# A two-layer attention kernel: its matmuls cut into narrow column tiles

## The chip, the cores and the metric

The kernel runs on one core of a Trainium2 chip. The metric is the device time of one launch, in microseconds. A core has five engines that run side by side and wait for each other by semaphores: TensorE multiplies matrices (in the profile PE for the matmuls and PEld for the loads of their stationary operands), VectorE (DVE), ScalarE (ACT) and GpSimd (POOL) work element by element, and SyncE (SP) starts transfers. A matmul computes lhsT.T @ rhs: lhsT is the stationary operand, loaded first, and rhs the moving one, streamed past it. TensorE's array has 128 rows (the contraction) and 128 columns (the output partitions). A matmul that needs fewer rows or columns can be placed in a part of the array. "128x32" in this text is such a tile: 128 rows by 32 columns. [...]

## The reference

The input x has 128 rows (called s) of 256 tokens with 256 channels each, in float32. Two layers are applied, each as x = x + attention(groupnorm(x)), with attention inside each row s.

```python
# layer 0: 8 heads of 32 channels
bias = einsum('nijz,zh->nhij', pair_repr, bias_proj)
gate = sigmoid(x @ gate_proj)
q, k, v = split(x @ qkv_proj, 3)
sim = softmax(q @ k.T * scale) + bias
out = ((sim @ v) * gate) @ out_proj
# layer 1: 4 heads of 64 channels, keys within 16 of the query only
q, k, v = split(x @ w_in.T + b_in, 3)
scores = where(|i - j| <= 16, q @ k.T / sqrt(64), -inf)
out = (softmax(scores) @ v) @ w_out.T + b_out
```

The group norm before each layer has 32 groups, and its mean and variance are taken over all rows, tokens and the group's channels, so layer 1 can't begin before layer 0 has finished its last row.

## The kernel before, in words

The kernel holds a row as two halves of 128 channels by 256 tokens and computes with channels on partitions. It has three parts: a start that computes the pair bias and the statistics of x; layer 0; and layer 1. A guarded third path that computes everything again with shifted exponents is there for extreme inputs; it isn't entered with these inputs.

**Products of weights and rows.** A product of a 256x256 weight matrix with a row of 256 tokens is four 128x128 blocks over 256 columns. For the projections q, k, v and the gate of layer 0, and q, k and the output projection of layer 1, the kernel takes two rows together and needs seven block products instead of eight, with sums of weight blocks (`Quarters`) and sums of row blocks (`row_sums`). Class `Seven` (L573) does this in layer 0, and `two_of_them` (L616) interleaves two of them, q with k or v with gate, over one row stage each. Class `Summed` (L648) does it in layer 1, and `in_turn` (L687) interleaves q, k and the output projection of an earlier row pair. Both come through `product` at L594, or at L598 for v of layer 0, where the row is the stationary operand and the weights move. `one_by_one` (L702) is the plain four-block product, used for the output projection of layer 0 (po) and for the last rows of layer 1.

**Layer 0, one row stage** (the loop over s at L913): `scores(s, 0)` (L777) multiplies keys with queries for four heads, each in 32 rows of the array, with 128 keys as columns; `sum_heads` (L822) sums the exponents of the previous row (zs) and multiplies the bias with the values (bv); `attend` (L853) multiplies the exponents with the values (av); both go through `products` (L808) as 128x32 tiles, a head each. Then come `scores(s, 1)` for the other four heads and a `stretch` (L885) with 14 block products of the next row pair and the four of po. ScalarE takes the exponents and copies projections out of PSUM, VectorE forms sums, the reciprocal, the norm of rows to come and the residual, GpSimd the block sums.

**Layer 1, one stage of two rows** (the loop at L1256): `scores` (L1055) for both rows in 64x64 tiles, each with 64 keys and the 96 queries near them; `attend` (L1086) multiplies with the values, also 64x64, and sums the exponents into zs with `place` (L979) as 64x32 tiles; `stretch` (L1022) has 21 block products; `values` (L1037) computes v for two rows to come, in 128x64 tiles of 64 tokens. `sums` (L1125) copies the two half sums and adds them; `inverse` takes the reciprocal in three pieces between other VectorE work; `by_transfer` (L1146) sends it to DRAM and back, spread over partitions (1near); `divide` (L1170) multiplies it in (1at).

**What sets the order.** In both layers the order on TensorE, ScalarE and VectorE is that of the program (a manual schedule), in layer 1 also on GpSimd and SyncE. A float32 matmul appears in the profile as two loads and two matmuls, so every count on TensorE is twice that of the calls. [...]in layer 0 five form a ring that projections and scores share (`psum(banks0, "0", 5, 0)`), in layer 1 four, beside two for av and two for zs.

Of the kernel before, what the change touches and what calls it, by code (L numbers as in the profile page):

```python
# [9 lines left out]
F32 = mybir.dt.float32  # L10
AF = mybir.ActivationFunctionType
ALU = mybir.AluOpType
# [27 lines left out]
def conv_preact_kernel(  # L40
# [59 lines left out]
    def strip(a):  # L100
        return slice(B * a, B * (a + 1))
# [464 lines left out]
    def row_sums(t, x, engine):  # L566
# [3 lines left out]
        engine.tensor_tensor(t[:, 2], x[:, 3], x[:, 2], ALU.subtract)  # L570
        engine.tensor_tensor(t[:, 3], x[:, 1], t[:, 1], ALU.subtract)

    class Seven:  # L573


        def __init__(self, pool, weights, x, t, name, tag, by_token=False):
            self.weights, self.x, self.t, self.by_token, self.name = weights, x, t, by_token, name
# [7 lines left out]
        def product(self, n, two=None, first=False):  # L585
            x, t = self.x, self.t
            moving = {1: x[:, 0], 2: x[:, 1], 3: x[:, 3], 4: t[:, 3], 5: t[:, 0], 6: t[:, 1], 7: t[:, 2]}[n]
            out = two if n == 2 else self.ps[:, 1 if n in (3, 5) else 0, :]

            first = first or n == 1  # L590
            flags = dict(stop=n in (2, 3, 4), skip_group_check=True)
            weights = self.weights.stationary(n)
            if not self.by_token:
                nc.tensor.matmul(out, lhsT=weights, rhs=moving, start=first, **flags)  # L594
                return
            for t2 in range(2):
                cols = slice(t2 * P, (t2 + 1) * P)
                nc.tensor.matmul(out[:, cols], lhsT=moving[:, cols], rhs=weights, start=first and t2 == 0, **flags)  # L598

        def take(self, what):  # L600
            if what == "15":
# [44 lines left out]
            p.add_mid()  # L646

    class Summed(Seven):  # L648

# [47 lines left out]
            if n in (1, 5):  # L699
                amid(n)  # L700

    def one_by_one(w, at, name, done):  # L702

        ps = proj_bank(name)
        done(ps)
        for m in range(2):
            for kt in range(2):
                nc.tensor.matmul(  # L708
                    ps[:, m, :], lhsT=w[:, kt, m * P : (m + 1) * P], rhs=at[:, kt, :],
                    start=(kt == 0), stop=(kt == 1),  # L710
                )
                yield
# [10 lines left out]
    with ExitStack() as both:  # L723
# [20 lines left out]
        with ExitStack() as lay0:  # L744
# [32 lines left out]
            def scores(s, half):  # L777
                i, r = divmod(s, 2)
                q, k = res["q", i], res["k", i]
                sims = [sim_bank(f"sim{s}_{half}_{j}") for j in range(4)]  # L780
                for kt in range(2):
                    for j in range(4):
                        p0 = D0 * j
                        nc.tensor.matmul(  # L784
                            sims[j][:, kt, :],
                            lhsT=k[p0 : p0 + D0, 2 * r + half, kt * P : (kt + 1) * P],
                            rhs=q[p0 : p0 + D0, 2 * r + half, :],
                            start=True, stop=True,
                        )
                ex = att.tile([P, 4, 2, R], F32, tag="ex", name=f"ex{s}_{half}", bufs=4)  # L790
                both = att.tile([P, 4, R], F32, tag="both", name=f"both{s}_{half}")
                hd[s, half] = (ex, both)


                def weigh(js):
                    for j in js:
                        nc.scalar.activation(ex[:, j], sims[j], AF.Exp, scale=1.0 / math.sqrt(D0))  # L797

                weigh(range(3))
                return lambda: weigh((3,))  # L800
# [84 lines left out]
            def stretch(names, i, s, rest=lambda: None):  # L885

                po = iter(())
                if s >= 0:
                    po = one_by_one(out_sb, st[s]["at"], f"po{s}", lambda ps: st[s].update(po=ps))
                if 2 * i >= S:  # L890
                    rest()
                    for _ in po:
                        pass
                    return
                f, g = (
                    Seven(row, quarters[w], xns[i], tss[i], f"{w}{i}", w, by_token=(w == "v")) for w in names
                )
                for w, p in zip(names, (f, g)):
                    res[w, i] = p.to
                two_of_them(row, f, g, f"{names}{i}", po, rest)  # L900


            with tc.manual_schedule(engines={mybir.EngineType.PE, mybir.EngineType.Activation, mybir.EngineType.DVE}):
# [54 lines left out]
                for s in (S - 2, S - 1):  # L958
                    if s == S - 1:
                        keep_on(4)  # L960
                    for _ in one_by_one(out_sb, st[s]["at"], f"po{s}", lambda ps: st[s].update(po=ps)):
                        pass
                    finish(s)
                mean1, rstd1 = channel_columns(st1, most1, 1, keep_on)
# [4 lines left out]


        with ExitStack() as lay:
            ps_av = psum(lay, "1", 4, 0)
            row = lay.enter_context(tc.tile_pool(name="row1", bufs=4))
            att = lay.enter_context(tc.tile_pool(name="att1", bufs=2))
            st, hd, outs = {s: {} for s in range(S)}, {}, {}
# [38 lines left out]
            def project(s):  # L1014

                if s < 0:
                    return iter(())
                return one_by_one(w_out_t, st[s]["at"], f"1po{s}", lambda ps: st[s].update(po=ps))

            ats, ats_t, outputs, last_ots = {}, {}, {}, {}  # L1020

# [15 lines left out]
            def values(s):  # L1037
                if s >= S:
                    return
                i, r = divmod(s, 2)  # L1040
                ps = proj_bank(f"p1v{s}").rearrange("p a (b c) -> p (a b) c", c=P)
                for b in range(NB):
                    for kt in range(2):
                        for half in range(2):
                            nc.tensor.matmul(  # L1045
                                ps[KB * half : KB * (half + 1), b, :],
                                lhsT=xns[i][:, 2 * r + kt, KB * b : KB * (b + 1)],
                                rhs=w_in_t[:, kt, 2 * C + P * half : 2 * C + P * (half + 1)],
                                start=(kt == 0), stop=(kt == 1),
                            )  # L1050
                v = row.tile([P, NB, P], F32, tag="v", name=f"1v{s}")
                nc.scalar.copy(v, ps)  # L1052
                st[s]["v"] = v
# [32 lines left out]
            def attend(i):  # L1086

                if i < 0:
                    return

                if i < S // 2 - 1:
                    av = ps_av.tile([P, 2, 2, R], F32, tag="av", name=f"1av{i}", bufs=1)
                    av = [av[:, half] for half in range(2)]
                else:
                    av = [proj_bank(f"1av{i}_{half}") for half in range(2)]
                zs = ps_av.tile([P, 2, 2, R], F32, tag="zs", name=f"1zs{i}", bufs=1)
                zps = []
                for r in range(2):
                    (p, zp), v = hd.pop(2 * i + r), st[2 * i + r]["v"]
                    zps.append(zp)  # L1100
                    for b in range(NB):
                        for half in range(2):
                            for j in range(2):
                                keys, cols = slice(KB * half, KB * (half + 1)), slice(D1 * j, D1 * (j + 1))
                                q0, p0 = QLO[b], R * (b % 2) + QLO[b]

                                nc.tensor.matmul(  # L1107
                                    av[half][cols, r, q0 + QIN[b].start : q0 + QIN[b].stop],
                                    lhsT=v[keys, b, cols],
                                    rhs=p[keys, j, p0 + QIN[b].start : p0 + QIN[b].stop],  # L1110
                                    start=(r == 0 and b == 0), stop=(b == NB - 1),
                                    skip_group_check=True,
                                )

                for r in range(2):
                    for half in range(2):
                        for j in range(2):
                            keys = slice(KB * half, KB * (half + 1))
                            nc.tensor.matmul(
                                zs[strip(2 * j + r), half, 0, :], lhsT=place[keys, :], rhs=zps[r][keys, j, :],  # L1120
                                start=True, stop=True,
                            )
                hd["av", i] = (av, zs)

            def sums(i):  # L1125
                if i < 0:
                    return
                zs = hd["av", i][1]
                z = att.tile([P, R], F32, tag="z", name=f"1z{i}")
                nc.scalar.copy(z, zs[:, 0, 0, :])  # L1130
                nc.vector.tensor_tensor(z, zs[:, 1, 0, :], z, ALU.add)
                rz = att.tile([P, R], F32, tag="rz", name=f"1rz{i}")
                near = att.tile([P, 2, 2, R], F32, tag="near", name=f"1near{i}", bufs=1)
                hd["z", i] = (z, rz, near)
# [388 lines left out]
```

## Time and profile before

| | |
|---|---|
| Time before, median of 3 runs | 3169.02 us (3168.06 to 3169.51) |
| Span of the profiled execution | 3173.6 us |
| Instructions | 87,645, of them 36,859 matmuls and as many weight loads |
| Busy: PE, PEld | 98%, 75% |
| Busy: DVE, ACT, POOL | 81%, 59%, 51% |
| Mean granted TensorE clock | 0.991 |
| Row stages of layer 0 | from about 240 to 2080 us of the span |
| Stages of layer 1 | from about 2110 to 3145 us |

The profile is of one execution, whose own time is its span; it is 4.6 us longer than the median of the runs. A line of the timeline gives the start, the length, the engine, the source line, the operation, the output and its inputs, the rows and columns of the array that it uses, the shape of the moving operand and the count. Lengths of matmuls overlap, since a matmul starts before the one ahead has left the array; the time that a block takes is therefore read from its start to the next block's start.

### The profile page before, as it was taken

To read this page: it belongs to the slowest core of one execution; us is meant where nothing else is said; L and a number is where in the kernel's file an instruction comes from. 1 tells how busy PE (TensorE), PEld (TensorE's weight loads), DVE (VectorE), ACT (ScalarE), POOL (GpSimd) and SP (SyncE) were. 2 spreads that over 40 slices of the span, in tenths; PEclk is the share of its full clock that TensorE was granted. 3 is DMA by queue.
4 is the path that set the end of the run, shared out by engine and by line. 5 is a ranking of instruction groups with operands and counts; after the bars stand their busy time and mean duration, and the time that the engine had idled before them with its cause. 6 is when DMAs were issued, how large, how long until landed. Compare 5 with 4: busy or idle time off the path is not lost.

```text
span 3173.6 us, 87645 instructions
## 1 busy us (share of the span) xinstructions
PE 3097.4 (98%) x36859; PEld 2384.0 (75%) x36859; DVE 2558.2 (81%) x4140; ACT 1870.3 (59%) x4064; POOL 1613.4 (51%) x1651
## 2 busy tenths in 40 slices
PE   7889999999999999999999999999999999999997
PEld 5567777777777777777777777768888888888886
DVE  4669999999999999999999999956666666666665
ACT  4656666666666666666666666645555555555553
POOL 3034444444444444444444444347777777777774
PEclk8989999999999999999999999999999999999999
DMA  9931111111111111111111111004444444444343
GB/s 379 424 109 42 41 41 34 41 35 39 37 35 41 35 39 37 38 38 35 41 34 37 39 37 39 28 28 102 96 101 101 93 99 102 100 97 101 91 100 69
DMA packets 357105, 242.44 MB, mean 76 GB/s; under 512 B 276072, under 2 KB 342112, under 8 KB 350560
## 3 DMA queue, kind: packets, MB, share of 16 engines
q1 hardware_dynamic: 355808, 234.39, 27.1%
q8 instruction: 292, 4.78, 0.6%
q0 software_dynamic: 752, 2.36, 0.2%
q14 instruction: 109, 0.89, 0.1%
q10 hardware_dynamic: 144, 0.00, 0.0%
HBM read 169.09 MB, written 67.62 MB: 75 GB/s over the span
## 4 chain that ended last, share of the span: by engine, by line
PE 91%; DMA 5%; DVE 2%; ACT 1%; issue 0%; POOL 0%; SPq 0%; DVEq 0%; POOLq 0%; ACTq 0%
PE sim L784 9%; PE p1v L1045 7%; PE po L708 7%; PE av L816 7%; PE bv L816 7%; PE p1q L594 6%; PE pv L598 6%; PE p1o L594 6%; PE pq L594 6%; PE p1k L594 6%; PE pk L594 5%; PE pg L594 5%; DMA pr<-in_L_conv_pair_repr_dram 4%; PE zs L830 4%; PE 1sim L1066 3%; PE 1av L1107 3%
## 5 line engine op out<-in xcount | busy, mean ns | idle before, releaser
L797 ACT ACTIVATE ex<-sim 128x512 f32<-128x512 f32 x1024 | 547.5, 605 | 429.9 <-PE sim L784 429.9
L806 DVE TENSOR_TENSOR both<-ex 128x512 f32<-128x512 f32 x512 | 483.9, 984 | 77.0 <-ACT ex L797 77.0
L846 DVE RECIPROCAL d<-d 128x512 f32<-128x512 f32 x128 | 429.2, 3353 | 4.4
L611 POOL TENSOR_TENSOR v<-v,twovg 128x256 f32<-128x256 f32 x64 | 75.4, 1179 | 548.0 <-ACT twovg L630 548.0
L784 PE MATMUL sim<-q,k 32*128 32x256 f32 x4096 | 295.7, 401 | 1.1 <-ACT ex L797 1.1
L708 PE MATMUL po<-at,out_sb 128*128 128x256 f32 x1024 | 285.0, 382 | 4.0 <-DVE at L864 4.0
L784 PEld LDWEIGHTS sim<-q,k 32*128 32x128 f32 x4096 | 186.7, 184 | 102.4 <-issue 95.0
L816 PE MATMUL bv<-bias_sb,v 128*32 128x256 f32 x4096 | 244.5, 379 | 0.7 <-DVE t L861 0.7
L816 PE MATMUL av<-ex,v 128*32 128x256 f32 x4096 | 244.5, 379 | 0.0
L1045 PEld LDWEIGHTS p1v<-w_in_t,1xn 128*64 128x64 f32 x4096 | 222.3, 137 | 21.5 <-PE p1k L594 20.2
L1045 PE MATMUL p1v<-w_in_t,1xn 128*64 128x128 f32 x4096 | 237.7, 274 | 0.3 <-POOL place L980 0.3
L1076 POOL TENSOR_TENSOR 1p<-1ex,seen 128x768 f32<-128x768 f32 x127 | 230.9, 1818 | 13.4 <-ACT 1ex L1074 13.4
L668 ACT ACTIVATE 1q<-p1q,bqk 128x256 f32<-128x256 f32 x192 | 91.1, 474 | 244.4 <-PE p1q L594 244.4
L708 PEld LDWEIGHTS po<-at,out_sb 128*128 128x128 f32 x1024 | 185.7, 191 | 25.4 <-issue 4.3
L1176 DVE TENSOR_TENSOR 1at<-1av,1near 128x512 f32<-128x512 f32 x128 | 82.6, 686 | 148.6 <-DMA 1near<-rz_far 116.7
L816 PEld LDWEIGHTS bv<-bias_sb,v 128*32 128x32 f32 x4096 | 133.2, 110 | 88.7 <-issue 1.1
L611 POOL TENSOR_TENSOR q<-q,twoqk 128x256 f32<-128x256 f32 x64 | 47.6, 744 | 298.5 <-ACT twoqk L630 298.5
L816 PEld LDWEIGHTS av<-ex,v 128*32 128x32 f32 x4096 | 133.2, 110 | 87.8 <-issue 0.3
L766 DVE TENSOR_SCALAR xn<-xt,mean,rstd 128x256 f32<-128x256 f32 x256 | 179.9, 742 | 0.0
L1083 POOL TENSOR_TENSOR 1zp<-1p 128x512 f32<-128x512 f32 x127 | 162.1, 1276 | 10.0
L568 POOL TENSOR_TENSOR 1ts<-1xn 128x256 f32<-128x256 f32 x64 | 47.0, 734 | 234.3 <-ACT 1xn L1006 234.3
L1052 ACT COPY 1v<-p1v 128x512 f32<-128x512 f32 x128 | 75.1, 587 | 135.1 <-PE p1v L1045 131.6
(300 smaller groups left out, 7872.4 us busy)
## 6 DMA issues: line engine op xcount, KB each, us to landing
pr<-in_L_conv_pair_repr_dram SPq DMA_DIRECT2D x32, 1024.0 KB
xs<-in_x_dram SPq DMA_DIRECT2D x16, 2048.0 KB
x<-o SPq DMA_DIRECT2D x64, 512.0 KB
yg<-x SPq DMA_DIRECT2D x64, 512.0 KB
out_dram<-1o SPq DMA_DIRECT2D x256, 128.0 KB
xg<-in_x_dram SPq DMA_DIRECT2D x252, 128.0 KB
1near<-rz_far SPq DMA_DIRECT2D x124, 256.0 KB
rz_far<-1rz SPq DMA_DIRECT2D x124, 4.0 KB
```

Source lines behind the costliest of these rows:

```text
L594: nc.tensor.matmul(out, lhsT=weights, rhs=moving, start=first, **flags)
L598: nc.tensor.matmul(out[:, cols], lhsT=moving[:, cols], rhs=weights, start=first and t2 == 0, **flags)
L708: nc.tensor.matmul(ps[:, m, :], lhsT=w[:, kt, m * P : (m + 1) * P], rhs=at[:, kt, :], start=(kt == 0), stop=(kt == 1),)
L766: nc.vector.tensor_scalar(xns[i][:, 2 * r + half, :], xt[:, half, :], mean0[:, half : half + 1], rstd0[:, half : half + 1], op0=ALU.subtra ...
L784: nc.tensor.matmul(sims[j][:, kt, :], lhsT=k[p0 : p0 + D0, 2 * r + half, kt * P : (kt + 1) * P], rhs=q[p0 : p0 + D0, 2 * r + half, :], sta ...
L797: nc.scalar.activation(ex[:, j], sims[j], AF.Exp, scale=1.0 / math.sqrt(D0))
L806: nc.vector.tensor_tensor(both[:, j : j + 2], ex[:, j : j + 2, 0, :], ex[:, j : j + 2, 1, :], ALU.add)
L816: nc.tensor.matmul(to[D0 * j : D0 * (j + 1), half, :], lhsT=v[:, 2 * r + half, c0 : c0 + D0], rhs=weights(4 * half + j, kt), start=(kt == ...
L846: nc.vector.reciprocal(d, d)
L1045: nc.tensor.matmul(ps[KB * half : KB * (half + 1), b, :], lhsT=xns[i][:, 2 * r + kt, KB * b : KB * (b + 1)], rhs=w_in_t[:, kt, 2 * C + P * ...
L1076: engine.tensor_tensor(p.rearrange("p j (r c) -> p (j r) c", c=WROW)[:, :, 0 : 2 * WSTEP] .rearrange("p r (t c) -> p r t c", c=WSTEP)[:, : ...
L1083: engine.tensor_tensor(zp, p[:, :, 0:R], p[:, :, R : 2 * R], ALU.add)
```

## The change

All products of weights and rows in both layers are issued as four matmuls of 32 columns each, one after another, instead of one of 128 columns. A new function does it, and `Seven.product`, hence also `Summed`, and `one_by_one` call it with a width of 32 (`B`).

```diff
+    def in_columns(out, lhsT, rhs, width, **flags):
+        for c0 in range(0, P, width):
+            cols = slice(c0, c0 + width)
+            nc.tensor.matmul(out[cols], lhsT=lhsT[:, cols], rhs=rhs, **flags)
...
             if not self.by_token:
-                nc.tensor.matmul(out, lhsT=weights, rhs=moving, start=first, **flags)
+                in_columns(out, weights, moving, self.WIDTH, start=first, **flags)
                 return
...
-                nc.tensor.matmul(out[:, cols], lhsT=moving[:, cols], rhs=weights, start=first and t2 == 0, **flags)
+                in_columns(out[:, cols], moving[:, cols], weights, self.WIDTH, start=first and t2 == 0, **flags)
...
-                nc.tensor.matmul(
-                    ps[:, m, :], lhsT=w[:, kt, m * P : (m + 1) * P], rhs=at[:, kt, :],
+                in_columns(
+                    ps[:, m, :], w[:, kt, m * P : (m + 1) * P], at[:, kt, :], width,
                     start=(kt == 0), stop=(kt == 1),
                 )
```

The scores of layer 0 take 64 keys as columns instead of 128, so that eight tiles of 32x64 fill the array where four of 32x128 did.

```diff
                 for kt in range(2):
-                    for j in range(4):
-                        p0 = D0 * j
-                        nc.tensor.matmul(
-                            sims[j][:, kt, :],
-                            lhsT=k[p0 : p0 + D0, 2 * r + half, kt * P : (kt + 1) * P],
+                    for c in range(2):
+                        for j in range(4):
+                            p0, k0 = D0 * j, kt * P + KB * c
+                            nc.tensor.matmul(
+                                sims[j][KB * c : KB * (c + 1), kt, :],
+                                lhsT=k[p0 : p0 + D0, 2 * r + half, k0 : k0 + KB],
```

In layer 1 the values take 32 tokens as columns instead of 64, and the sums of the exponents use all 128 rows at once, with both halves of the keys, so that the addition of two half sums on VectorE goes. The sums then need one bank of PSUM instead of two, and the ring for projections and scores has five banks instead of four. The scores and the products with the values in layer 1 stay 64x64.

```diff
-            ps_av = psum(lay, "1", 4, 0)
+            ps_av = psum(lay, "1", 5, 0)
...
-                        for half in range(2):
+                        for n in range(A):
+                            half, keys = n // 2, KB * b + B * (n % 2)
                             nc.tensor.matmul(
-                                ps[KB * half : KB * (half + 1), b, :],
-                                lhsT=xns[i][:, 2 * r + kt, KB * b : KB * (b + 1)],
+                                ps[strip(n), b, :],
+                                lhsT=xns[i][:, 2 * r + kt, keys : keys + B],
...
-                zs = ps_av.tile([P, 2, 2, R], F32, tag="zs", name=f"1zs{i}", bufs=1)
+                zs = ps_av.tile([P, 2, R], F32, tag="zs", name=f"1zs{i}", bufs=1)
...
-                    for half in range(2):
-                        for j in range(2):
-                            keys = slice(KB * half, KB * (half + 1))
-                            nc.tensor.matmul(
-                                zs[strip(2 * j + r), half, 0, :], lhsT=place[keys, :], rhs=zps[r][keys, j, :],
-                                start=True, stop=True,
-                            )
+                    for j in range(2):
+                        nc.tensor.matmul(
+                            zs[strip(2 * j + r), 0, :], lhsT=place, rhs=zps[r][:, j, :], start=True, stop=True
+                        )
...
-                nc.scalar.copy(z, zs[:, 0, 0, :])
-                nc.vector.tensor_tensor(z, zs[:, 1, 0, :], z, ALU.add)
+                nc.scalar.copy(z, zs[:, 0, :])
```

More of the change, by code (lines that the diff above doesn't have):

```diff
@@ L571, in row_sums @@
         engine.tensor_tensor(t[:, 3], x[:, 1], t[:, 1], ALU.subtract)
+    def in_columns(out, lhsT, rhs, width, **flags):
+        for c0 in range(0, P, width):
+            cols = slice(c0, c0 + width)
+            nc.tensor.matmul(out[cols], lhsT=lhsT[:, cols], rhs=rhs, **flags)
     class Seven:
+        WIDTH = B
         def __init__(self, pool, weights, x, t, name, tag, by_token=False):
@@ L648, in conv_preact_kernel @@
     class Summed(Seven):
+        WIDTH = B
         def __init__(self, pool, weights, x, t, name, tag, bias=None, y=None):
@@ L700, in in_turn, with one_by_one @@
                 amid(n)
-    def one_by_one(w, at, name, done):
+    def one_by_one(w, at, name, done, width):
         ps = proj_bank(name)
@@ L781, in scores @@
                 for kt in range(2):
-                    for j in range(4):
-                        p0 = D0 * j
-                        nc.tensor.matmul(
-                            sims[j][:, kt, :],
-                            lhsT=k[p0 : p0 + D0, 2 * r + half, kt * P : (kt + 1) * P],
-                            rhs=q[p0 : p0 + D0, 2 * r + half, :],
-                            start=True, stop=True,
-                        )
+                    for c in range(2):
[4 more added lines that the diff above has]
+                                lhsT=k[p0 : p0 + D0, 2 * r + half, k0 : k0 + KB],
+                                rhs=q[p0 : p0 + D0, 2 * r + half, :],
+                                start=True, stop=True,
+                            )
                 ex = att.tile([P, 4, 2, R], F32, tag="ex", name=f"ex{s}_{half}", bufs=4)
@@ L888, in stretch @@
                 if s >= 0:
-                    po = one_by_one(out_sb, st[s]["at"], f"po{s}", lambda ps: st[s].update(po=ps))
+                    po = one_by_one(out_sb, st[s]["at"], f"po{s}", lambda ps: st[s].update(po=ps), B)
                 if 2 * i >= S:
@@ L960, in conv_preact_kernel @@
                         keep_on(4)
-                    for _ in one_by_one(out_sb, st[s]["at"], f"po{s}", lambda ps: st[s].update(po=ps)):
+                    for _ in one_by_one(out_sb, st[s]["at"], f"po{s}", lambda ps: st[s].update(po=ps), B):
                         pass
@@ L1017, in project @@
                     return iter(())
-                return one_by_one(w_out_t, st[s]["at"], f"1po{s}", lambda ps: st[s].update(po=ps))
+                return one_by_one(w_out_t, st[s]["at"], f"1po{s}", lambda ps: st[s].update(po=ps), B)
             ats, ats_t, outputs, last_ots = {}, {}, {}, {}
@@ L1115, in attend @@
                 for r in range(2):
-                    for half in range(2):
-                        for j in range(2):
-                            keys = slice(KB * half, KB * (half + 1))
-                            nc.tensor.matmul(
-                                zs[strip(2 * j + r), half, 0, :], lhsT=place[keys, :], rhs=zps[r][keys, j, :],
-                                start=True, stop=True,
-                            )
+                    for j in range(2):
+                        nc.tensor.matmul(
+                            zs[strip(2 * j + r), 0, :], lhsT=place, rhs=zps[r][:, j, :], start=True, stop=True
+                        )
                 hd["av", i] = (av, zs)
```

## The prediction

> **What bounds the kernel now.** I read the page first. Its busy shares and its chain of work that ended last name one engine:
>
> ```profile
> PE 3097.4 (98%) x36859; PEld 2384.0 (75%) x36859; DVE 2558.2 (81%) x4140; ACT 1870.3 (59%) x4064; POOL 1613.4 (51%) x1651
> ...
> PE 91%; DMA 5%; DVE 2%; ACT 1%; issue 0%; POOL 0%; SPq 0%; DVEq 0%; POOLq 0%; ACTq 0%
> ```
>
> TensorE carries 91% of the chain, so the question is what its time consists of. The timeline of TensorE in one row stage of layer 0 (start, us, engine, line, operation, tiles, rows*columns of the array used, moving operand, count) shows it:
>
> ```profile
> 1009.32 1.03 PE L708 MATMUL po<-at,out_sb 128*128 128x256 f32 x4
> 1010.28 1.15 PE L784 MATMUL sim<-q,k 32*128 32x256 f32 x16
> 1011.35 1.07 PE L830 MATMUL zs<-both,ones 128*32 128x256 f32 x16
> 1012.24 1.91 PE L816 MATMUL bv<-bias_sb,v 128*32 128x256 f32 x32
> 1013.97 1.91 PE L816 MATMUL av<-ex,v 128*32 128x256 f32 x32
> 1015.81 1.15 PE L784 MATMUL sim<-q,k 32*128 32x256 f32 x16
> 1016.88 0.71 PE L598 MATMUL pv<-qkv_sb,xn 128*128 128x128 f32 x4
> 1017.43 0.61 PE L598 MATMUL pv<-sums_v,ts 128*128 128x128 f32 x4
> 1017.88 0.60 PE L594 MATMUL pg<-xn,gate_sb 128*128 128x256 f32 x2
> ```
>
> Start to start, bv takes 1.73 us for 32 instructions: 8 groups of four 128x32 tiles, 0.216 us a group. In the same timeline a pair of 128x128 matmuls over 256 columns takes 0.43, so 0.216 each. Four narrow tiles run side by side in the time of one wide one; the split by itself costs and gains nothing in the array.
>
> What is left over sits at the seams. Start to start less 0.216 per full pass: po 0.96-0.863 = 0.097; sim 1.07-0.863 = 0.207; zs 0.89-0.863 = 0.027; bv 0; av 1.84-1.728 = 0.112; sim 0.207; the first pv 0.55-0.437 = 0.113. The sum is 0.76 us of a stage of 14.63 (29.26 per two rows). Each change of tile shape costs an exit of about 0.10 and an entry that follows the stationary width: 0.11 for 128 columns, 0.03 for 32.
>
> Layer 1, same view, one stage of two rows (16.37 us):
>
> ```profile
> 2403.22 0.64 PE L594 MATMUL p1o<-1att,sums_1o 128*128 128x256 f32 x2
> 2403.69 0.59 PE L594 MATMUL p1q<-1ts,sums_1q 128*128 128x256 f32 x2
> ...
> 2407.19 0.59 PE L594 MATMUL p1o<-1at,sums_1o 128*128 128x256 f32 x2
> 2407.71 3.71 PE L1045 MATMUL p1v<-w_in_t,1xn 128*64 128x128 f32 x64
> 2411.36 1.56 PE L1066 MATMUL 1sim<-1q,1k 64*64 64x96 f32 x61
> ...
> 2414.14 0.66 PE L1119 MATMUL 1zs<-1zp,place 64*32 64x256 f32 x16
> 2414.74 0.70 PE L594 MATMUL p1q<-1xn,w_in_t 128*128 128x256 f32 x2
> 2415.27 0.59 PE L594 MATMUL p1k<-1xn,w_in_t 128*128 128x256 f32 x2
> ```
>
> Left over: last p1o 0.52-0.43 = 0.09; p1v 3.65-3.49 (32 groups of 0.109) = 0.155; 1zs 0.60-0.432 = 0.168; first p1q 0.53-0.43 = 0.10; two p1o pairs 0.47-0.43 = 0.04 each, where a weight load waited for VectorE. Scores and products (2.78 us) share one shape and stay as they are.
>
> Could another engine take over? VectorE is closest in layer 0:
>
> ```profile
> 1000.00:1438.80 438.80, 438.80 (x4656) 327.72 (x4650) 410.67 (x481) 280.66 (x585) 195.13 (x181) 1.00 0.15 37
> ```
>
> The columns after the length are busy PE, PEld, DVE, ACT, POOL. VectorE works 410.67 of 438.80, so 0.94 us of each stage is free. In layer 1 a DMA is close:
>
> ```profile
> DVE 1at L1176 <- DMA 1near<-rz_far: 37.4, 17, 3.3
> ```
>
> That is from the waits over 20 stages. By the starts in the trace, 1at ends 0.15 us before the next 1av, the least possible, in 11 of 63 stages, 0.2 to 0.5 before it in 17, and 0.7 or more in 35.
>
> [...]
>
> **The change part by part.**
>
> Layer 0 keeps four changes of shape a stage, but 128x128 becomes 128x32 and 32x128 becomes 32x64. Exits from 128x32 are av's, 0.112; entries to it zs's, 0.027. No row shows 32x64. Lower bound: 32 columns and a four-tile exit, 0.03+0.09 = 0.12 per sim block; upper bound: 128 columns with an eight-tile exit (1zs: 0.168-0.027 = 0.14), 0.25. I take 0.05 for 64 columns (p1v's 0.155 less an exit of 0.10) and the eight-tile exit 0.14, since now eight tiles start one after another: 0.19. The stage then pays 2x0.19 + 2x0.112 + 2x0.027 = 0.66 instead of 0.76: 0.10 less, x127 = 12.7 us (bounds +30 and -2). The by-token products take 0.44 to 0.45 per four where the array needs 0.437[...]: about 0.056 per two rows, x64 = 3.6 us. Layer 0: **16 us**.
>
> Layer 1: products, values and sums now have one shape, so a stage has two changes instead of four. Gone are 0.09 (p1o's exit), p1v's entry 0.05, the exit of 1zs 0.14 and p1q's entry 0.10; p1v's exit becomes av's, 0.01 dearer. The sums issue 8 instructions of 0.054 instead of 16 of 0.027, the same 0.43. Net 0.37. The two p1o gaps: [...]between 0 and 0.08, I take 0.04. 0.41 x 63 = **26 us**. The values double to 128 instructions, still 0.109 per group of four.
>
> The VectorE add of two half sums goes (0.42 x 63). VectorE isn't the bound, so that is worth nothing, except that the chain sums, reciprocal, transfer, 1at starts a little earlier; but the last reciprocal stands behind p1o's fifth product on VectorE, so it moves with TensorE. The chain is fixed from there to 1at, while TensorE shortens that part by about 0.17 (values' entry and exits). In the 11 stages without room this is lost: 11x0.17, with the tight ones 2.2 us. So layer 1 gives 24. The fifth bank of the ring frees nothing: waits for banks show 1 to 2 us in the whole run. Outside the loop, narrow projections of the last rows now alternate with wide products of `spread`: a few seams, under 1 us, left out of the sum.
>
> New waits: none is added by name. A product's consumer waits for four tiles, the last starting 21 ns later (7 ns apart in the trace). In layer 0 the closest consumer chain is `at` to po: at ends 0.8 to 1.1 us before the load, and TensorE's gain inside that stretch is 0.10.
>
> Sum: 16+24 = 40. Against its own span the changed kernel is profiled at 3173.6-40 = 3133.6; the runs' median is 4.6 lower, 3169.0, so **3129**.
>
> **The rivals.**
>
> (a) Instructions can't be fetched fast enough: slower. Matmuls go from 36,859 to 69,133 by my count, loads alike. The page's instruction queue moved 4.78 MB in 292 packets, 16 KB each; that becomes about 548. In layer 1 the values, scores and products take 512 instructions in 6.3 us, two packets, which take 1.13 us each in the trace. For it: nothing before sustained this. Against: scores and products alone already take 256 in 2.78 us without a gap. It decides at 40/548 = 73 ns lost per packet; one packet in three late by 0.5 us is 91 us: 3220.
>
> (b) Four tiles reading the very same moving rows slow each other: slower too. In bv each tile has its own rows; no row of before shows four tiles on one. About 8,200 full passes are split so; 10 ns each is 82: 3211. It decides at 4.9 ns. Against: bv's four streams also read the same partitions at once, 7 ns apart, and take no longer than one.
>
> (c) The transfer in layer 1 binds in every stage: all 63 lose 0.17, 10.7 instead of 2.2: 3137.
>
> (d) The 32x64 scores are no cheaper (upper bound): layer 0 gives about 2 instead of 16: 3143. For it: four changes per stage remain.
>
> **How the numbers follow.** Forecast 0.70, (a) 0.06, (b) 0.07, (c) 0.06, (d) 0.08, and 0.03 for none of them. The forecast's own range is 3114 to 3141: the p1o gaps at both ends (2.5 us each way) and the 32x64 cost most of the way to either bound (10 to 12 us). Three runs differed by 1.5 us, and 0.2% (6 us) is about what a measurement can tell from no change. Forecast, (c) and (d) are faster; (a) and (b) are slower, save small doses of either that end near zero. Faster 0.83, same 0.05, slower 0.12. Leaving out (a), (b) and the far end of (d), the range is 3112 to 3158.
>
> **What would show it.** In the changed timeline, p1q, p1k and p1o run on from 1zs with 0.216 per group of four and no 0.10 at p1v; the layer 1 stage is 15.95 to 16.0. sim blocks take about 1.05 and the row stage 14.50. Wrong by (a): idle TensorE put down to issue in the middle of products; by (b): groups above 0.216; by (c): 1av waiting for VectorE in most stages; by (d): sim start to start 1.11.

## The result, and the profile after

The changed kernel takes 3202.0 us (median of 4 runs, 3197.8 to 3212.3) against 3169.3 (3168.1 to 3170.9): 1.0104 of the time before, interval 1.0086 to 1.0122. It is 33 us slower; 3129 was forecast. Its profiled execution has a span of 3201.1 us, 27.5 more than that of before.

The page of the changed kernel, by the same lines as before, with that of the instruction queue (packets, MB, share of the DMA engines):

```profile
PE 3075.1 (96%) x69133; PEld 1984.6 (62%) x69133; DVE 2519.4 (79%) x4076; ACT 1871.3 (58%) x4064; POOL 1626.6 (51%) x1651
...
q8 instruction: 544, 8.91, 1.2%
...
PE 91%; DMA 5%; issue 2%; DVE 2%; ACT 1%; POOL 0%; SPq 0%; DVEq 0%; POOLq 0%; ACTq 0%
```

The count of matmuls is the forecast one, 69,133, and the instruction packets are 544 instead of 292 (about 548 were forecast). TensorE's busy time fell by 22 us, and yet the kernel is slower. In the chain, issue (time in which an engine waits for nothing that the profile shows) went from 0% to 2%, which is the first hint of where the time went.

Layer 0 did what was forecast. TensorE's timeline in a row stage:

```profile
1011.68 1.05 PE L577 MATMUL po<-at,out_sb 128*32 128x256 f32 x16
1012.65 1.12 PE L794 MATMUL sim<-q,k 32*64 32x256 f32 x32
1013.70 1.07 PE L840 MATMUL zs<-both,ones 128*32 128x256 f32 x16
1014.59 1.91 PE L826 MATMUL bv<-bias_sb,v 128*32 128x256 f32 x32
1016.32 1.91 PE L826 MATMUL av<-ex,v 128*32 128x256 f32 x32
1018.16 1.12 PE L794 MATMUL sim<-q,k 32*64 32x256 f32 x32
1019.21 0.64 PE L577 MATMUL pq<-xn,qkv_sb 128*32 128x256 f32 x8
1019.66 0.61 PE L577 MATMUL pq<-ts,sums_q 128*32 128x256 f32 x8
```

From start to start the sim blocks take 1.05 where they took 1.07, the entry after them 0.45-0.432 = 0.02 where it was 0.11, and a product of 8 instructions 0.43 as before. A stage (half of the median of two rows) fell from 14.63 to 14.48 us.

Layer 1 is where the time went. Its stage grew from 16.44 to 17.34 us in the mean (the middle 60 of 63), though two changes of shape are gone from it. The timeline shows a stage with two gaps, the idle time ahead of a line in brackets:

```profile
2430.24 3.70 PE L1056 MATMUL p1v<-w_in_t,1xn 128*32 128x128 f32 x128
2433.88 0.46 PE L1077 MATMUL 1sim<-1q,1k 64*64 64x96 f32 x9
2436.19 1.30 PE L1077 MATMUL 1sim<-1q,1k 64*64 64x96 f32 x52 [1.85 <-issue]
...
2438.71 0.64 PE L1128 MATMUL 1zs<-1zp,place 128*32 128x256 f32 x8
2440.13 0.64 PE L577 MATMUL p1q<-1xn,w_in_t 128*32 128x256 f32 x8 [0.78 <-issue]
2440.56 0.64 PE L577 MATMUL p1k<-1xn,w_in_t 128*32 128x256 f32 x8
```

TensorE stops in the middle of the scores, after 9 of 64 matmuls with the same inputs and outputs (three of the 64 come a little later, among the 1av), and again ahead of a product whose rows have long been there. No engine releases it. From 1zs to p1q, where no gap stands, the step is 0.45 (another stage: 2420.41 to 2420.86), so the change of shape there costs what was forecast. The waits of TensorE over the whole run (us in total, times, longest) sort the long gaps by where they fall:

```profile
PE 1sim L1077 <- issue: 22.1, 26, 1.9
PE 1av L1118 <- issue: 12.9, 25, 1.0
PE p1v L1056 <- issue: 5.7, 12, 0.7
```

They lie in the values, the scores and the products with the values, or just behind them: the stretch with the most instructions per microsecond. Numbering TensorE's instructions (loads, matmuls and the semaphore instructions between them) in order of their starts gives the cause a name. Between 2120 and 3080 us, 75 loads or matmuls start over 0.36 us after the one before. At all 75 the pause ends with an instruction whose number leaves 193 when divided by 256 (74 times the load or matmul itself, once a semaphore instruction just ahead of it), and each time the last packet of 16 KB had landed 1.2 to 1.7 us before. Over the whole run 138,940 instructions are numbered, 255 for each of the 544 packets, so a packet stands for 256. TensorE had run out of instructions. By the time in which it got through the 256 instructions of a block, with the mean gap ahead of the next block:

```
us for 256 instructions   before: blocks, mean gap   changed: blocks, mean gap   block + gap
2.5 to 3.0                12, 0.01                   15, 0.80                    3.68
3.0 to 3.3                 4, 0.00                   27, 0.75                    3.91
3.3 to 3.6                 5, 0.09                   20, 0.88                    4.36
3.6 to 4.5                11, 0.08                   34, 0.64                    4.5
4.5 to 5.0                 5, 0.09                   23, 0.15                    4.86
over 5.0                  86, 0.05                   84, 0.03
```

Before, a single block of 2.6 us passes without a gap: the block ahead of each of the 12 blocks of 2.5 to 3.0 us took over 13 us. In the changed kernel the block ahead of such a one took 4.0 us (median), and the block after it is late. The packets' own times show how. In the kernel before, the packet for the next block starts 0.2 us before the first instruction of such a dense block (mean); in the changed kernel it starts 1.1 us after it. With 1.1 us of transfer and 1.2 from landing to the first instruction that makes 3.4, the shortest time seen from one waited-for block to the next. The gaps at every 256th instruction add up to 69 us in 56.6 stages, 1.22 a stage. Without them the mean stage of 17.34 would be 16.12, 0.32 less than before.

In layer 1 of both kernels no packet starts more than 0.5 us before the block ahead of its own begins (at the earliest 0.45 us before it in the kernel before, 0.39 us after it in the changed one). So while a block ran, no more than the next one had landed. Two blocks that were waited for, one right behind the other, start 3.4 to 3.7 us apart at the least (3.40 to 3.72 in 13 of 22 such pairs of the changed kernel).

### The profile page after: what moved, and what is told of

It reads as the page before. It is cut to its first block, busy times and chain, and to the rows that moved or that the text cites. A ratio compares the mean times of both kernels' runs of the same rounds, so it can differ in the third digit from the quotient of the medians.

```text
span 3201.1 us, 153013 instructions
## 1 busy us (share of the span) xinstructions
PE 3075.1 (96%) x69133; PEld 1984.6 (62%) x69133; DVE 2519.4 (79%) x4076; ACT 1871.3 (58%) x4064; POOL 1626.6 (51%) x1651
## 4 chain that ended last, share of the span: by engine, by line
PE 91%; DMA 5%; issue 2%; DVE 2%; ACT 1%; POOL 0%; SPq 0%; DVEq 0%; POOLq 0%; ACTq 0%
PE sim L794 8%; PE p1v L1056 7%; PE po L577 7%; PE av L826 7%; PE bv L826 7%; PE p1q L577 6%; PE p1o L577 6%; PE p1k L577 6%; PE pv L577 5%; PE pq L577 5%; PE pk L577 5%; PE pg L577 5%; PE zs L840 4%; PE 1sim L1077 3%; DMA pr<-in_L_conv_pair_repr_dram 3%; PE 1av L1118 3%
## 5 line engine op out<-in xcount | busy, mean ns | idle before, releaser
L577 PE MATMUL po<-at,out_sb 128*32 128x256 f32 x4096 | 291.9, 381 | 4.1 <-DVE at L874 4.1
L794 PE MATMUL sim<-q,k 32*64 32x256 f32 x8192 | 288.0, 387 | 1.2 <-ACT ex L807 1.2
L1151 DVE RECIPROCAL 1rz<-1z 128x64 f32<-128x64 f32 (+1 forms) x192 | 129.7, 678 | 180.7 <-ACT 1z L1138 180.7
L1056 PE MATMUL p1v<-w_in_t,1xn 128*32 128x128 f32 x8192 | 243.1, 273 | 6.3 <-issue 5.7
L1056 PEld LDWEIGHTS p1v<-w_in_t,1xn 128*32 128x32 f32 x8192 | 231.0, 110 | 18.8 <-issue 10.4
L794 PEld LDWEIGHTS sim<-q,k 32*64 32x64 f32 x8192 | 151.9, 131 | 126.6 <-issue 79.4
L577 PEld LDWEIGHTS po<-at,out_sb 128*32 128x32 f32 x4096 | 131.1, 110 | 71.3 <-issue 5.2
L775 DVE TENSOR_SCALAR xn<-xt,mean,rstd 128x256 f32<-128x256 f32 x256 | 160.8, 667 | 0.0
```

Source lines behind the costliest of these rows:

```text
L577: nc.tensor.matmul(out[cols], lhsT=lhsT[:, cols], rhs=rhs, **flags)
L775: nc.vector.tensor_scalar(xns[i][:, 2 * r + half, :], xt[:, half, :], mean0[:, half : half + 1], rstd0[:, half : half + 1], op0=ALU.subtra ...
L794: nc.tensor.matmul(sims[j][KB * c : KB * (c + 1), kt, :], lhsT=k[p0 : p0 + D0, 2 * r + half, k0 : k0 + KB], rhs=q[p0 : p0 + D0, 2 * r + ha ...
L1056: nc.tensor.matmul(ps[strip(n), b, :], lhsT=xns[i][:, 2 * r + kt, keys : keys + B], rhs=w_in_t[:, kt, 2 * C + P * half : 2 * C + P * (half ...
L1151: nc.vector.reciprocal(rz[:, cols], z[:, cols])
```

## The experiments

The theory (A): TensorE's instructions come too late in the dense stretch of layer 1. Its rivals: narrow tiles themselves are dear, above all where four share their moving rows (B), or the transfer of the reciprocals binds (C).

**Each layer's part alone.** Against the changed kernel, the first has layer 1 whole as before (its values, sums, ring and `project` too), the second layer 0 (its scores and po too).

```diff
     class Summed(Seven):
-        WIDTH = B
+        WIDTH = P
```

```diff
     class Seven:
-        WIDTH = B
+        WIDTH = P
```

> Layer 0's part of the change alone; layer 1 as before. Theory A (in layer 1 instructions reach TensorE too late): layer 0 has no such dense stretch, so its seams give their gain in full: about 19 to 23 us faster than before, near 3148. Theory B (four tiles on the same moving rows slow each other, or narrow tiles cost more than they look): slower than before, or at best equal, since layer 0 issues most of these tiles.

> Layer 1's part of the change alone; layer 0 as before. Theory A: the whole loss is here: about 0.88 us a stage over 62 stages, 54 us slower, near 3223, and the long gaps of TensorE all fall on the same place of every 256th instruction. Theory C (the transfer of the reciprocals binds): the same time, but then the products with the values wait for VectorE and not for nothing.

Layer 0 alone: 3151.3 us, 0.9943 of the time before (0.9926 to 0.9960), 18 us faster. Layer 1 alone: 3219.5 us, 1.0157 (1.0140 to 1.0174), 50 us slower. The two add up to the result. Theory B is out: layer 0, with more than half of all split passes, gains. In layer 1 alone 73 of 77 gaps over 0.36 us between 2120 and 3080 us fall on the 256th instructions; the other four lie between 2120 and 2125, at its start. Its products with the values don't wait for VectorE (they start within 0.2 us of the end of 1at in 4 of 55 stages only), so theory C is out as the cause too.

**The smallest edit that brings the loss.** The kernel before, with one change:

```diff
-                        for half in range(2):
+                        for n in range(A):
+                            half, keys = n // 2, KB * b + B * (n % 2)
                             nc.tensor.matmul(
-                                ps[KB * half : KB * (half + 1), b, :],
-                                lhsT=xns[i][:, 2 * r + kt, KB * b : KB * (b + 1)],
+                                ps[strip(n), b, :],
+                                lhsT=xns[i][:, 2 * r + kt, keys : keys + B],
```

> The kernel before with one edit, layer 1's values in tiles of 32 tokens instead of 64: 128 more instructions of TensorE a stage, the same array time, the same number of changes of shape. Theory A: values, scores and products are now 512 instructions in 6.3 us, as in the changed kernel, so TensorE runs dry at the end of them: 0.3 to 0.9 us a stage, 20 to 55 us slower, 3190 to 3225. Theories B and C: within 5 us of before, since no new tile shares its rows with three others (two do) and the transfer is untouched.

3219.3 us, 1.0153 (1.0136 to 1.0170): 50 us, as much as all of layer 1's edits together, near the top of what theory A expected, from 128 more instructions a stage, with the array's work and the number of seams unchanged. Its waits are those of the changed kernel:

```profile
PE 1sim L1067 <- issue: 18.2, 24, 1.5
PE 1zs L1120 <- issue: 4.8, 6, 1.1
PE 1av L1108 <- issue: 4.5, 13, 0.6
```

**The same instructions in another order.** The changed kernel, values inside the stretch of products:

```diff
                         if n == 5:
                             by_transfer(i - 1)
+                        values(s + 2 if n == 1 else s + 3)
...
                     bounds(i - 1)
-                    values(s + 2)
-                    values(s + 3)
```

> The changed kernel with the same instructions in another order: the values of the two rows stand inside the stretch of products (after its first and its fifth round) instead of behind it, so that no stretch of more than 256 instructions is dense. Theory A: most of the 1.2 us a stage comes back; the scores now follow the last products at once and may wait 0.2 to 0.3 us for their banks; 3120 to 3160, faster than before. Theories B and C: no gain over the changed kernel, about 3200.

3188.0 us, 1.0052 (1.0036 to 1.0069), slower than expected. The relief came, and most of it was taken by a new wait. The gaps at the 256th instructions fell from 69 to 14 us over the same stretch of layer 1 with the same 864 instructions a stage, so density counts, not number. But TensorE's waits now begin with another line:

```profile
PE 1av L1118 <- DVE 1at L1183: 39.3, 48, 2.4
...
PE 1av L1118 <- issue: 7.8, 14, 1.3
```

1av overwrites the banks that the division before it (1at) reads, so it must wait for that division. Between the last product and 1av now stand only the scores, 1.4 us, where 3.6 us of values stood too. In 55 of 56 stages 1av starts within 0.2 us of the end of 1at, and 59 us pass in all between the last of the scores and 1av, 3.5 in the changed kernel. The transfer has a part in it, theory C's wait called up by the cure: it is issued after product 5 (the order is 2, 1, 5, 6, 7, 4, 3), with the values of one row now ahead of it, and VectorE idles ahead of 1at for 20 us in all, 14 of them put down to the transfer. The larger part is VectorE's own order: the additions for the last products, then 1.3 us of division, which the values no longer cover.

```diff
-            if n in (1, 5):
+            if n in (1, 5, 7):
                 amid(n)
...
+                        if n > 1:
+                            values(s + 2 if n == 5 else s + 3)
```

> The changed kernel with the values inside the stretch, but later than in the last order: after the fifth and after the seventh product's round, behind the issue of the reciprocals' transfer. Theory A: the same relief of the instruction supply as in the first spread order (14 us of gaps at the 256th instructions in 980 us instead of 69), and the products with the values no longer wait for the transfer, as it has the time of all values again: 3132 to 3155. If the wait in the first spread order had another cause than the late transfer, this stays near 3188.

3156.9 us, 0.9951 (0.9935 to 0.9968), just outside the upper end. In this second order the values stand after products 5 and 7. Moved behind the issue of the transfer, the same values cost 31 us less, and the gaps at the 256th instructions stayed small (9.5 us in 960). But 32 us in 960 still pass between the last of the scores and 1av. The transfer has no part in these: VectorE goes from the additions of the last product into the division without a wait in every stage, and 1av starts within 0.2 us of its end in 55 of 58:

```profile
2440.84 0.63 PE L577 MATMUL p1o<-1at,sums_1o 128*32 128x256 f32 x8
2441.40 1.55 PE L1077 MATMUL 1sim<-1q,1k 64*64 64x96 f32 x64
2443.29 1.61 PE L1118 MATMUL 1av<-1p,1v 64*64 64x80 f32 x64 [0.34 <-POOL 1ts L569]
...
2441.53 0.43 DVE L694 TENSOR_TENSOR 1o<-p1o,mid1o 128x256 f32<-128x256 f32 x1
2441.87 1.28 DVE L1183 TENSOR_TENSOR 1at<-1av,1near 128x512 f32<-128x512 f32 x2
```

The profile puts the wait down to GpSimd's 1ts, which ended last; 1av doesn't use it. The division ends at 2443.15.

**Fewer instructions in layer 1.** Two ways, layer 0 as in the changed kernel. Both put the values back into 64-token tiles, as before; the first also has the products and `project` in tiles of 64 columns:

```diff
     class Summed(Seven):
-        WIDTH = B
+        WIDTH = KB
```

> The changed kernel with layer 1's products and values in tiles of 64 columns; its sums stay 128x32, layer 0 is the changed one. 568 instructions of TensorE a stage instead of 864 (500 before), three changes of shape instead of two (four before), and none dearer. Theory A: no long gaps, a stage of 16.1 to 16.2 us: 3132 to 3140. If column tiles of any width are what hurts layer 1: near 3200.

> The changed kernel with layer 1's values alone back in 64-token tiles: 736 instructions a stage, four changes of shape. Theory A: only scores and products are dense, and the gaps at the 256th instructions mostly go: 3132 to 3155. If the number of instructions of a whole stage counted and not their density: half of the 50 us stay, 3170 to 3180.

Both beat both kernels: 3131.6 us, 0.9876 (0.9859 to 0.9892), and 3131.0 us, 0.9871 (0.9855 to 0.9888). The second keeps 736 instructions a stage and one more seam than the changed kernel, three in all (its expectation counted four). Its timeline has no gap, and its stage takes 16.09 us (median), near the 15.95 to 16.0 forecast for the change:

```profile
2412.65 3.71 PE L1055 MATMUL p1v<-w_in_t,1xn 128*64 128x128 f32 x64
2416.29 1.55 PE L1076 MATMUL 1sim<-1q,1k 64*64 64x96 f32 x64
2417.66 1.39 PE L1117 MATMUL 1av<-1p,1v 64*64 64x80 f32 x64
2418.99 0.64 PE L1127 MATMUL 1zs<-1zp,place 128*32 128x256 f32 x8
2419.44 0.61 PE L577 MATMUL p1q<-1xn,w_in_t 128*32 128x256 f32 x8
```

Ten of its blocks took 2.5 to 3.0 us, and their mean gap is 0.005: scores and products with the values alone (256 instructions, from 2416.29 to 2418.99) are still served.

**Half of it.** The values of one row in 64-token tiles, those of the other in 32:

```diff
                     for kt in range(2):
+                        if r == 0:
+                            for half in range(2):
+                                nc.tensor.matmul(
+                                    ps[KB * half : KB * (half + 1), b, :],
+                                    lhsT=xns[i][:, 2 * r + kt, KB * b : KB * (b + 1)],
...
+                            continue
```

> The changed kernel with the values of the first row of each pair in 64-token tiles and those of the second in 32: the dense run before the sums is 128+256 = 384 instructions instead of 512 (no loss was seen at 256, 0.9 to 1.2 us a stage at 512). If about one block of 256 is held ahead and the loss grows with what a dense run has beyond it: a quarter to a half of the 71 us between the two, 3148 to 3168. If any 32-token values bring the loss: near 3200; if only a full second block does: near 3131.

3149.9 us, 0.9934 (0.9917 to 0.9950), 19 more than with all values wide. About half is one more seam, between the two rows' values (from the first of the values to the scores 3.78 us pass instead of 3.64, 8 us in 58 stages), and about half, 9 us, lies at the 256th instructions (11.2 against 2.3). So the first 128 instructions beyond a block of 256 cost about 9 us in 960, and the next 128 bring it to 69. The loss doesn't grow evenly.

**Is it the other transfers that make instructions late?** The changed kernel, with seven of eight stores left out:

```diff
                     o = outs.pop(s // 2)
+                    if s < S - 1 and (s // 2) % 8:
+                        return
```

> The changed kernel that stores only every eighth row pair of layer 1 and leaves the rest of the output unwritten: most of the 128 KB stores (in pieces of 256 bytes) are gone. If these transfers, on the same DMA engines, lengthen the instruction packets' way: the gaps shrink from 1.2 to 0.5 to 0.8 us a stage and the time to 3160 to 3180. If the supply is slow by itself, 3.4 us and more for 256 instructions: 3190 to 3202.

3193.7 us, 1.0074 (1.0057 to 1.0090): 8 us of the 71 between the changed kernel and values_wide, and its interval still touches that of the changed kernel. The windows of both, changed kernel first (length; busy PE, PEld, DVE, ACT, POOL; clock; DMA share; GB/s):

```profile
2300.00:2627.60 327.60, 312.38 (x8151) 221.01 (x8146) 196.69 (x434) 165.94 (x396) 221.53 (x226) 1.00 0.40 95
```

```profile
2300.00:2627.60 327.60, 314.15 (x8276) 223.24 (x8271) 197.99 (x437) 168.15 (x401) 225.12 (x229) 1.00 0.25 68
```

The DMA engines' share fell from 0.40 to 0.25, and the gaps from 1.22 to 1.13 us a stage. These stores are not what makes the supply slow; the transfers that stay weren't varied. The packet's own transfer takes 1.03 to 1.11 us (median, layer 1) in all these runs; the other 2.3 us of the shortest distance pass before it starts (1.05 at the least) and after it has landed (1.2 at the least).

**Layer 0's gain, split.** The first experiment with the scores back in 32x128:

```diff
-                    for c in range(2):
-                        for j in range(4):
-                            p0, k0 = D0 * j, kt * P + KB * c
+                    for j in range(4):
+                        p0 = D0 * j
```

> Layer 0's products in 128x32 tiles, its scores back in 32x128, layer 1 as before: it splits layer 0's gain of 18 us. By the seams read before, a stage pays 2x0.112+2x0.207+2x0.027 = 0.69 us instead of 0.76, and the by-token products save their 3.6 us: 12 to 13 us faster than before, near 3157; the 32x64 scores are then worth the other 5 to 6. If the scores' tiles carry the gain: 3165.

3157.1 us, 0.9958 (0.9944 to 0.9972). The narrow products bring about 12 of layer 0's 18 us and the 32x64 scores about 6, as expected.

```profile
1030.37 1.15 PE L793 MATMUL sim<-q,k 32*128 32x256 f32 x16
1031.45 1.07 PE L839 MATMUL zs<-both,ones 128*32 128x256 f32 x16
```

A 32x128 block takes 1.07 to 1.08 between narrow neighbours, where the 32x64 block takes 1.05.

## Why the prediction was wrong

- **What bounds the kernel: right.** TensorE did, and its time was full passes plus seams. The seams could be read from start to start.
- **A split pass costs nothing in the array: right.** Groups of four 128x32 tiles take 0.216 us also with the same moving rows (a product of 8 instructions takes 0.43). Rival (b) is refuted.
- **Layer 0, 16 us: right.** 18 us. The 32x64 blocks cost 0.19 over their passes, the value taken between the bounds. The by-token products (pv, p2vg) take 0.437 from start to start where they took 0.444 to 0.446 (medians), so that gain came too; what held them before isn't shown.
- **Layer 1's seams, 0.41 us a stage: right in kind, too high.** The time outside the 256th instructions fell by 0.32. Two terms didn't come. The values still take 3.63 us up to the scores (3.64 before), so the 0.05 for their entry stayed. So did the 0.04 for the two p1o gaps: rounds with p1o still show steps of 0.46 to 0.47. The loads did get shorter, about 110 ns for 32 columns where 128 took 190; that the gaps would shrink with them was the author's estimate.
- **The failed step: "The values double to 128 instructions, still 0.109 per group of four."** It charged instructions nothing beyond the array. In the changed kernel 512 instructions in 6.3 us outrun the supply, which costs 1.22 us a stage, some 76 us over 63 stages. The values' edit alone, put into the kernel before, costs 50.
- **Rival (a) was the case, at 0.06.** Its price was sound: more than 73 ns per packet decides; 76 us over 544 packets are 140. What misjudged it was the argument against: 256 instructions in 2.78 us ran without a gap, so the supply was taken to keep up. That one block had been fetched while a slow one of over 13 us ran, and the packet behind it had started early too, 0.2 us before it. The question was what happens with a second dense one behind it, and no row of before had two.
- **The transfer in layer 1, 2.2 us: not seen as a cost.** In values_wide, with its shorter stage, 1av waited for 1at once in 20 stages, 0.4 us. But the room there was as small as said: reordering for the instructions' sake made 1av wait for the division, and the transfer held that up for a third of the time at most.
- **The sum.** 40 us of gain was forecast, and 40 came in values_wide (3131.0 against 3171.1 beside it), which has all of the change but its dense values. That the sums agree is in part chance: values_wide keeps a change of shape whose removal was forecast at 0.14 us a stage, 9 us. By the traces its layer 0 gave 18.5 us and the stages of layer 1 gave 19, not 24; a few more came outside both loops.

Still open is what fills the 2.3 us around a packet's transfer, and why the loss grows so unevenly from 384 to 512 dense instructions.

## What to carry to other kernels

Splitting a matmul into narrow column tiles to avoid changes of shape is worth it by the seams (0.10 us an exit, 0.03 to 0.11 an entry here), but each split multiplies instructions, and these have a supply of their own (here 1.22 us a stage were lost to it). Count loads and matmuls per microsecond over stretches of two blocks of 256: where more than one block in a row takes under some 3.7 us (an estimate from the distances and means above), split less, or put slower work between, and check what the moved work stood ahead of and what it covered. A gap called issue that returns at every 256th instruction is the sign.

## What the runs showed of the hardware that was not expected

- TensorE's instructions come in packets of 16 KB, 256 at a time; the transfer takes 1.03 to 1.11 us, the first instruction starts 1.2 us or more after it has landed, and blocks that are waited for start at least 3.4 to 3.7 us apart, 3.7 to 4.5 in the means above. No packet starts more than 0.5 us before the block ahead of its own begins: behind a block of over 13 us one of 2.6 us passed without a gap, behind one of 4.0 us (median) the block after the dense one came 0.80 us late (mean).
- The supply hardly depends on the stores: with most of them left out and the DMA share at 0.25 instead of 0.40, the gaps fell by 7%.
- A block of 32x64 tiles, eight side by side, takes 1.05 us, 0.19 over its passes, where one of 32x128 tiles has 0.21. How the 0.19 divides between entry and exit isn't shown.
